# A graph attention layer: the first-tile rows of every batch gathered raw from x and projected in the loop, x and table moved in 4.6 KB pieces

## The chip, the cores and the metric

The kernel runs on one core of one Trainium2 chip. The metric is the device time of one execution in microseconds, the median of several runs. A core has five instruction streams: PE (TensorE, matmuls and transposes), DVE (VectorE), ACT (ScalarE), POOL (GpSimd, which issues the indirect gathers here) and SP (SyncE, which issues most plain DMAs). Each works through its own instructions in order; semaphores order them against each other. PEld in the profile is the loading of weights into TensorE, which runs beside its matmuls.

## The reference

One layer of a graph network with attention: 12,500 nodes of 128 values, 412,500 edges sorted by their target `dst`, 64 values per edge, 4 heads of 32.

```python
h = relu(layernorm(x))                               # per node, eps 1e-5
hn = (h @ W_node.T).reshape(num_nodes, 4, 32)
e = (edge_attr @ W_edge.T).reshape(num_edges, 4, 32)
att = sum(concat([hn[src], hn[dst], e]) * a, -1)     # per edge and head
att = where(att > 0, att, 0.2 * att)
m = maximum(segment_max(att, dst), 0)
ex = exp(att - m[dst])
denom = segment_sum(ex, dst) + (num_edges - deg)[:, None] * exp(-m)
out = x + segment_sum((ex / denom[dst])[:, :, None] * hn[src], dst)
```

All values are float32.

## The kernel before

**The table (the start of the program, lines 185 to 452).** Each node gets a row of 144 float32 in a DRAM table: per head 32 projected values, two ones and the source's part of the logit (35 columns, `AW`), then four target parts of the logit. The 98 tiles of 128 nodes are taken in groups of 3, 6, 9, 9 and so on (`XB = 9`), and each group in units of three tiles (`XS`). A group is loaded by SP (`load_rows`, L254, in the layout "(b p) d -> p b d", where one partition gets nine separate pieces of 512 bytes), measured on DVE (`bn_stats`, L272), normalized (`normalize`: ACT L307, but in the first two units of a group the third tile on DVE, L304), transposed on PE (L313), put through relu on DVE (L318), multiplied by the weights `wall` on PE (L323) and copied to `rows` by ACT (L330), while POOL sets the ones (L331). ACT issues the write of a whole group to the table (L335, 576-byte pieces). The order is written out by hand: in step k unit k is projected, unit k+2 normalized and turned, unit k+8 measured. After that come `extent` on DVE for the four groups of target indices (L236 to L240), eight small matmuls (L413) and a row of DVE operations that make per-chunk constants.

**The loop (lines 774 to 808).** The edges are cut into chunks of 7 tiles of 128 edges; 8 chunks make a batch, so a batch has 56 tiles, and there are 58 batches. Iteration b does, in this order of code:

- `index(b + 2)` and `load(b + 1)`: SP loads of the indices, the edge values `eft` (1,792 KB), the targets `mem` (896 KB) and eight small pieces `twb` of the table;
- `gather(b + 1)`: POOL first copies `sums` into `gate` (L507) and then issues 56 indirect gathers (L509), one per tile, which fetch 128 table rows each into the batch's `hs` buffer. There are two `hs` buffers, one for even and one for odd batches. `sums` is written by ACT (L623) out of the last PSUM group of a scatter, so the copy makes the gathers wait until the scatter that used this `hs` buffer is done;
- `weigh(b)`: when the batch's rows have landed, DVE and ACT turn logits into weights (L568 to L591);
- `scatter(b)`: DVE multiplies the rows by the weights (L605, eight times), PE sums them per target with one-hot matrices `hot` in three groups of chunks (L613: three, three and two chunks, 14 instruction records each) into two PSUM buffers `pa`, and ACT collects each group (L636, 12, 12 and 8 copies; L623 just before the last eight);
- `begin(b + 1)`: DVE compares targets (L536), PE computes the edge part `z` of the logits (L541, 16 records, and L545, 8), DVE makes `key` and `hot` (L549 to L560);
- `merge`, after every second batch: DVE (and two ACT exponentials) chain the collected chunks and add them into `acc` (L640 to L683), with the small PSUM tile `here` (L669, L670) on the way;
- once, at b = 3, `count_windows`, which uses DVE, four loads and four matmuls;
- after about every fourth batch `finish`: the finished nodes' results are normalized and added to x.

The order of the code is the order on each engine (`manual_schedule`): what stands later in this list runs later on its engine, and an instruction that waits holds up all that follow it on the same engine.

## Time and profile before

| what | us |
|---|---|
| median of three runs (lowest, highest) | 4809.41 (4808.47, 4812.89) |
| the profiled execution | 4815.92 |
| its span, first to last instruction | 4814.2 |
| mean granted TensorE clock | 0.643 of full speed |
| first gather of table rows | 74.10 |
| first and last L507 (there are 56) | 233.2, 4700.0 |

Busy times of the engines over the span:

```profile
PE 1946.2 (40%) x4305; PEld 658.6 (14%) x4305; DVE 1805.7 (38%) x3337; ACT 719.1 (15%) x2772; POOL 3073.5 (64%) x3333
```

A line of the groups view reads: source line, engine, operation, what is written and read, how often, then busy time in us and the mean of one in ns, then the time the engine was idle just before these instructions and what ended most of that. "issue" is a wait for nothing that the profile shows, "remote" one whose releaser it doesn't know. A line of the timeline reads: start, duration, engine, line, operation, and in brackets the idle time before it and its releaser. A stage, in what follows, is the time from one L507 to the next.

### The profile page before, as it was taken

To read this page: it belongs to the slowest core of one execution; us is meant where nothing else is said; L and a number is where in the kernel's file an instruction comes from. 1 tells how busy PE (TensorE), PEld (TensorE's weight loads), DVE (VectorE), ACT (ScalarE), POOL (GpSimd) and SP (SyncE) were. 2 spreads that over 40 slices of the span, in tenths; PEclk is the share of its full clock that TensorE was granted. 3 is DMA by queue.
4 is the path that set the end of the run, shared out by engine and by line. 5 is a ranking of instruction groups with operands and counts; after the bars stand their busy time and mean duration, and the time that the engine had idled before them with its cause. 6 is when DMAs were issued, how large, how long until landed. Compare 5 with 4: busy or idle time off the path is not lost.

```text
span 4814.2 us, 21409 instructions
## 1 busy us (share of the span) xinstructions
PE 1946.2 (40%) x4305; PEld 658.6 (14%) x4305; DVE 1805.7 (38%) x3337; ACT 719.1 (15%) x2772; POOL 3073.5 (64%) x3333
## 2 busy tenths in 40 slices
PE   5334343433344335343434443434334433443353
PEld 3111111111011111110111111111111111110012
DVE  6242434242334332433343333424342434242425
ACT  5111111110111111111111111111111111110111
POOL 3666666666666666666666666666666666666662
PEclk8566666666666656665656665666566756666666
DMA  6332433333333333333333333333343333333431
GB/s 189 90 88 73 118 79 100 80 103 78 100 83 101 83 95 84 100 79 100 83 95 88 91 88 94 85 94 89 88 95 79 100 80 99 78 104 76 103 81 51
DMA packets 227639, 440.72 MB, mean 92 GB/s; under 512 B 85394, under 2 KB 135566, under 8 KB 227502
## 3 DMA queue, kind: packets, MB, share of 16 engines
q0 software_dynamic: 103136, 237.83, 21.8%
q1 hardware_dynamic: 111038, 194.10, 13.4%
q10 hardware_dynamic: 13328, 7.36, 0.5%
q14 instruction: 100, 0.82, 0.1%
q8 instruction: 37, 0.61, 0.1%
HBM read 423.75 MB, written 15.29 MB: 91 GB/s over the span
## 4 chain that ended last, share of the span: by engine, by line
issue 29%; another core or an unknown queue 27%; PE 22%; DVE 12%; ACT 8%; DMA 1%; DVEq 0%; SPq 0%; ACTq 0%; POOL 0%
PE pa L613 13%; PE z L541 6%; ACT r L636 4%; PE z L545 3%; DVE up L580 2%; DVE m L582 2%; ACT up L749 1%; DVE z L576 1%; ACT a L577 1%; ACT both L586 1%; DVE acc L683 1%; DVE a L583 1%; DVE up L664 1%; DVE hs L605 1%
## 5 line engine op out<-in xcount | busy, mean ns | idle before, releaser
L509 POOL DMA_INDIRECT hs<-table,ends x3223 | 3054.4, 948 | 1037.3 <-issue 1008.5
L613 PE MATMUL pa<-hs,hot 128*96 128x420 f32 (+2 forms) x2526 | 967.1, 549 | 1606.8 <-issue 1184.7
L560 DVE TENSOR_TENSOR hot<-exr,key 128x448 f32<-128x448 f32 x231 | 137.4, 621 | 2460.3 <-remote 2136.4
L541 PE MATMUL z<-eft,wa 128*32 128x384 f32 (+1 forms) x928 | 587.0, 695 | 913.6 <-issue 913.6
L636 ACT COPY r<-pa 32x35 f32<-32x35 f32 x1842 | 385.0, 209 | 2782.7 <-remote 1965.1
L613 PEld LDWEIGHTS pa<-hs,hot 128*96 128x96 f32 (+2 forms) x2526 | 445.1, 181 | 2152.8 <-issue 2044.2
L605 DVE TENSOR_TENSOR hs<-hs,exr 128x924 f32<-128x924 f32 x461 | 476.8, 1102 | 0.0
L545 PE MATMUL z<-mem,twb 128*32 128x512 f32 x464 | 341.2, 826 | 268.1 <-issue 268.1
L507 POOL COPY gate<-sums 32x1 f32<-32x1 f32 x56 | 9.9, 177 | 567.4 <-ACT sums L623 543.0
L541 PEld LDWEIGHTS z<-eft,wa 128*32 128x32 f32 x928 | 104.4, 117 | 1325.4 <-issue 1325.4
L576 DVE TENSOR_TENSOR z<-z,zst 32x224 f32<-32x224 f32 x232 | 89.8, 387 | 162.0 <-PE z L545 74.1
L586 ACT ACTIVATE both<-a 32x224 f32<-32x224 f32 x232 | 89.9, 388 | 370.7 <-DVE a L583 186.7
L536 DVE TENSOR_TENSOR mem<-mem,exr 128x896 f32<-128x896 int32 x116 | 120.4, 1077 | 65.5 <-issue 48.1
L577 ACT ACTIVATE a<-z 32x224 f32<-32x224 f32 x232 | 80.3, 346 | 418.0 <-issue 274.1
L545 PEld LDWEIGHTS z<-mem,twb 128*32 128x32 f32 x464 | 61.2, 134 | 585.3 <-issue 563.3
L683 DVE TENSOR_TENSOR acc<-acc,a 128x70 f32 x461 | 108.5, 235 | 33.8 <-issue 14.5
L580 DVE TENSOR_TENSOR_SCAN up<-pen,z 32x896 f32<-32x896 f32 x58 | 117.0, 2017 | 2.0
L582 DVE TENSOR_TENSOR_SCAN m<-pen,up 32x896 f32<-32x896 f32 x58 | 116.4, 2007 | 2.0
L588 DVE SCALAR_TENSOR_TENSOR both<-pen,m 32x224 f32<-32x224 f32 x232 | 88.7, 382 | 7.1 <-issue 4.8
L749 ACT COPY up<-a 32x224 f32<-32x224 f32 x208 | 70.7, 340 | 33.6 <-issue 23.3
L578 DVE TENSOR_TENSOR z<-z,a 32x896 f32<-32x896 f32 x58 | 63.0, 1087 | 24.5 <-issue 12.6
L583 DVE TENSOR_TENSOR a<-z,m 32x896 f32<-32x896 f32 x58 | 62.5, 1078 | 2.0
(142 smaller groups left out, 726.0 us busy)
## 6 DMA issues: line engine op xcount, KB each, us to landing
eft<-in_ef SPq DMA_DIRECT2D x58, 1792.0 KB
mem<-in_dstc SPq DMA_DIRECT2D x58, 896.0 KB
hs<-table,ends POOLq DMA_INDIRECT x3223
twb<-table SPq DMA_DIRECT2D x464, 0.5 KB
pen<-pens SPq DMA_DIRECT2D x58, 112.1 KB
table<-rows ACTq DMA_DIRECT2D x9, 648.0 KB
xg<-in_x SPq DMA_DIRECT2D x13, 448.0 KB
out<-xg SPq DMA_DIRECT2D x13, 448.0 KB
```

Source lines behind the costliest of these rows:

```text
L509: by_itself(nc.gpsimd.indirect_dma_start(out=s.hs[:, i, :], out_offset=None, in_=table[:, :], in_offset=bass.IndirectOffsetOnAxis(ap=s.end ...
L541: nc.tensor.matmul(s.z[:, part], wa3[:, j, :], s.eft[:, j, part], start=(j == 0), stop=False)
L545: nc.tensor.matmul(s.z[:, part], twb[:, s.b % 2, k, :], s.mem[:, k, part], start=False, stop=(k == 1))
L560: nc.vector.tensor_tensor(hot[:, :, q0:q0 + 2, :].rearrange("p t q r -> p q t r"), rows_ps[:, None, None, :].to_broadcast([P, 2, T, W]), k ...
L576: nc.vector.tensor_tensor(grouped(s.z, g), grouped(s.z, g), zst[g * R:(g + 1) * R, :, :], op=OP.add)
L580: nc.vector.tensor_tensor_scan(up, s.pen[:, :CE], s.z, 0.0, op0=OP.add, op1=OP.max)
L582: nc.vector.tensor_tensor_scan(m[:, ::-1], s.pen[:, CE:0:-1], up[:, ::-1], 0.0, op0=OP.add, op1=OP.max)
L586: nc.scalar.activation(both[g * R:(g + 1) * R, 0, :, :], grouped(att, g), AF.Exp)
L605: nc.vector.tensor_tensor(rows, rows, ex_ps[:, :n, q * H:(q + 1) * H, None].to_broadcast([P, n, H, HB]), op=OP.mult)
L613: nc.tensor.matmul(pa[:v * W, :v * H * AW], hot[:, i, q0:q0 + v, :].rearrange("p q r -> p (q r)"), by_chunk[:, q0:q0 + v, i, :], start=(i ...
L636: nc.scalar.copy(to, pa[q * W:(q + 1) * W, k:k + AW])
L683: nc.vector.tensor_tensor(cols, cols, put[:, i0 + i, :, :], op=OP.add)
```

## The change

Tile number 2 (`FIRST`) of each batch is no longer gathered from the table in the loop: `gather` issues 55 gathers instead of 56. Instead POOL gathers, while the table is built, the raw x rows of that tile for all 58 batches into `xs`, with the host-made index array `ahead`. DVE measures them (`measure_drawn`) after the extents, and SP writes them to a DRAM buffer `drawn` in two halves. In the loop `load` brings one batch's 128 rows back; `normalize` (ACT, and a PE transpose) stands before `begin(b + 1)`, `project` (DVE relu and a matmul) behind it, and `keep_rows` (DVE) writes the rows into `hs` after the merge. The transposed tile, the projected rows and merge's `here` share one PSUM tile `spare`.

Around it: x is loaded and the table written in the layout "(p b) d -> p b d", where a partition gets nine neighbouring rows (4.6 KB of x); POOL's memsets of pens, rows and xg go to DVE, or are dropped; DVE normalizes one tile per group of nine instead of two; the target indices for `extent` are loaded later, at k = 24, and into two buffers.

```diff
@@ -56,6 +56,7 @@
 LOGIT = EROW * 4
+FIRST = 2
 EPS = 1e-5
@@ -106,6 +107,7 @@
     ends: bass.AP,
+    ahead: bass.AP,
     dstc: bass.AP,
@@ -123,6 +125,7 @@
     pens = dram.tile([NC2, CE + 1], F32, name="pens")
+    drawn = dram.tile([P, NBT, D], F32, name="drawn")
 
@@ -148,6 +151,9 @@
     wa3 = const.tile([P, SB, R], F32, name="wa3")
+    wall = const.tile([P, ROW], F32, name="wall")
+    drawn_rstd = const.tile([P, NBT], F32, name="drawn_rstd")
+    drawn_shift = const.tile([P, NBT], F32, name="drawn_shift")
     ext = const.tile([P, NG, 2], F32, name="ext")
@@ -188,6 +194,8 @@
     ):
+        which = p1.tile([P, NBT], I32, name="which")
+        nc.scalar.dma_start(which, ahead)
         wn = p1.tile([P, D], F32, name="wn")
@@ -214,25 +222,47 @@
         nc.gpsimd.memset(wa3, 0.0)
-        wall = p1.tile([P, ROW], F32, name="wall")
         nc.gpsimd.memset(wall, 0.0)
 
-        rises, pens_sb = [], []
-
-        def load_extents():
-            for g in range(NG):
+        pen_bufs = [p1.tile([P, CE + 1], F32, name=f"pen{g}") for g in range(NG)]
+        line = {what: p1.tile([P, NC2], F32, name=what) for what in ("low", "top", "off", "qn", "bm", "later", "last")}
+        xs = p1.tile([P, NBT, D], F32, name="xs")
+        for b in range(NBT):
+            nc.gpsimd.indirect_dma_start(
+                out=xs[:, b, :], out_offset=None, in_=x[:, :],
+                in_offset=bass.IndirectOffsetOnAxis(ap=which[:, b:b + 1], axis=0))
+
+        def keep_drawn(first, last):
+            nc.sync.dma_start(drawn[:, first:last, :], xs[:, first:last, :])
+
+        def measure_drawn():
+            stats = p1.tile([P, NBT, 2, 3], F32, name="drawn_stats")
+            for b in range(NBT):
+                nc.vector.bn_stats(stats[:, b, :, :].rearrange("p a b -> p (a b)"), xs[:, b, :])
+            tot = p1.tile([P, NBT, 2], F32, name="drawn_tot")
+            nc.vector.tensor_tensor(tot, stats[:, :, 0, 1:], stats[:, :, 1, 1:], op=OP.add)
+            dif = p1.tile([P, NBT], F32, name="drawn_dif")
+            nc.vector.tensor_tensor(dif, stats[:, :, 0, 1], stats[:, :, 1, 1], op=OP.subtract)
+            nc.vector.scalar_tensor_tensor(dif, dif, D / 4.0, dif, op0=OP.mult, op1=OP.mult)
+            nc.vector.tensor_tensor(dif, dif, tot[:, :, 1], op=OP.add)
+            nc.scalar.activation(drawn_rstd, dif, AF.Sqrt, bias=eps, scale=1.0 / D)
+            nc.vector.reciprocal(drawn_rstd, drawn_rstd)
+            nc.vector.scalar_tensor_tensor(drawn_shift, tot[:, :, 0], -0.5, drawn_rstd, op0=OP.mult, op1=OP.mult)
+
+        loaded = []
+
+        def load_extents(first, last):
+            for g in range(first, last):
                 n = min(P, NC2 - g * P)
-                dch = p1.tile([P, CE], I32, name=f"dch{g}")
+                dch = p1.tile([P, CE], I32, name="dch", bufs=2)
                 nc.sync.dma_start(dch[:n, :], dstc[g * P:g * P + n, :])
-                rise = p1.tile([P, CE - 1], I32, name=f"rise{g}")
-                pen = p1.tile([P, CE + 1], F32, name=f"pen{g}")
-                nc.gpsimd.memset(pen, -BIG)
-                rises.append((dch, rise))
-                pens_sb.append(pen)
+                loaded.append(dch)
 
...
             n = min(P, NC2 - g * P)
-            (dch, rise), pen = rises[g], pens_sb[g]
+            dch, pen = loaded[g], pen_bufs[g]
+            rise = p1.tile([P, CE - 1], I32, name="rise")
+            nc.vector.memset(pen[:, ::CE], -BIG)
             nc.vector.tensor_tensor(rise[:n, :], dch[:n, 1:], dch[:n, :CE - 1], op=OP.subtract)
@@ -251,10 +281,10 @@
             s.x = p2.tile([P, XB, D], F32, name="xg", bufs=5)
-            nc.sync.dma_start(s.x[:, :full, :],
-                              x[b0 * P:(b0 + full) * P, :].rearrange("(b p) d -> p b d", p=P))
+            s.order = "(p b) d -> p b d" if full == n else "(b p) d -> p b d"
+            nc.sync.dma_start(s.x[:, :full, :], x[b0 * P:(b0 + full) * P, :].rearrange(s.order, p=P))
             if full < n:
-                nc.gpsimd.memset(s.x[:, full, :], 0.0)
+                nc.vector.memset(s.x[:, full, :], 0.0)
                 rest = N - (b0 + full) * P
@@ -300,7 +330,7 @@
                 k = slice(u.i0 + i, u.i0 + i + 1)
-                if i == XS - 1 and u.i0 < 2 * XS:
+                if i == XS - 1 and u.i0 < XS:
                     nc.vector.tensor_scalar(u.hn[:, i, :], s.x[:, k, :].rearrange("p b d -> p (b d)"),
@@ -328,11 +358,11 @@
             nc.scalar.copy(rows, u.ph[:, :u.m, :])
-            nc.gpsimd.memset(rows[:, :, :EROW].rearrange("p b (h k) -> p b h k", h=H)[:, :, :, HD:HD + 2], 1.0)
+            nc.vector.memset(rows[:, :, :EROW].rearrange("p b (h k) -> p b h k", h=H)[:, :, :, HD:HD + 2], 1.0)
             return s if u is s.units[-1] else None
...
         def write(s):
-            nc.scalar.dma_start(table[s.b0 * P:(s.b0 + s.n) * P, :].rearrange("(b p) c -> p b c", p=P),
+            nc.scalar.dma_start(table[s.b0 * P:(s.b0 + s.n) * P, :].rearrange(s.order, p=P),
                                 s.rows[:, :s.n, :])
@@ -393,7 +423,9 @@
                 early = [index(b) for b in range(2)]
-                load_extents()
+            if k == 24:
+                load_extents(0, 2)
+                keep_drawn(0, NBT // 2)
             k += 1
@@ -406,17 +438,20 @@
             extent(g)
+            load_extents(g + 2, min(g + 3, NG))
+        keep_drawn(NBT // 2, NBT)
+        measure_drawn()
         pb = [pps.tile([P, NC2], F32, name=f"pb{k}", bufs=1) for k in range(2)]
...
                                  ident[:n, :n], start=True, stop=True)
-        low = p1.tile([P, NC2], F32, name="low")
+        low = line["low"]
         nc.vector.tensor_copy(low, pb[0])
-        top = p1.tile([P, NC2], F32, name="top")
+        top = line["top"]
         nc.vector.tensor_tensor_scan(top, low, low, 0.0, op0=OP.max, op1=OP.max)
-        off = p1.tile([P, NC2], F32, name="off")
+        off = line["off"]
         nc.vector.tensor_tensor(off, low, top, op=OP.is_lt)
@@ -465,6 +500,11 @@
     nc.scalar.copy(nid_ps, nid)
+
+    spare = ps.tile([P, 512], F32, name="here")
+    here_ps = spare[:, :MC * 2].rearrange("p (c j) -> p c j", j=2)
+    turned_ps = spare[:, MC * 2:MC * 2 + P]
+    row_ps = spare[:, MC * 2 + P:MC * 2 + P + ROW]
 
@@ -489,6 +529,8 @@
                 f"twb{s.b}", twb_sems, twb_done, s.b % 2)
+        s.drawn = work.tile([P, D], F32, name="drawn")
+        nc.sync.dma_start(s.drawn, drawn[:, s.b, :])
         s.hs = (work if s.b % 2 else even).tile([P, SB * CT, ROW], F32, name="hs")
@@ -497,7 +539,8 @@
                     if t < held[c]:
-                        s.tiles.append(i)
+                        if i != FIRST:
+                            s.tiles.append(i)
                     else:
@@ -510,6 +553,24 @@
                 f"rows{s.b}", row_sems, row_done, s.b % ROWSEMS)
+
+    def normalize(s):
+
+        both = work.tile([P, BUF], F32, name="m")
+        s.hn, s.hT = both[:, :D], both[:, D:2 * D]
+        nc.scalar.activation(s.hn, s.drawn, AF.Identity, scale=drawn_rstd[:, s.b:s.b + 1],
+                             bias=drawn_shift[:, s.b:s.b + 1])
+        nc.tensor.transpose(turned_ps, s.hn, ident)
+
+    def project(s):
+
+        nc.vector.tensor_scalar(s.hT, turned_ps, 0.0, None, op0=OP.max)
+        nc.tensor.matmul(row_ps, s.hT, wall, start=True, stop=True)
+
+    def keep_rows(s):
+
+        nc.vector.tensor_copy(s.hs[:, FIRST, :], row_ps)
+        nc.vector.memset(s.hs[:, FIRST, :EROW].rearrange("p (h k) -> p h k", h=H)[:, :, HD:HD + 2], 1.0)
 
@@ -666,7 +727,7 @@
         put = work.tile([P, BUF], F32, name="a")[:, :MC * 2 * AW].rearrange("p (c j d) -> p c j d", c=MC, j=2)
-        here = ps.tile([P, MC, 2], F32, name="here")[:, :n, :]
+        here = here_ps[:, :n, :]
         nc.vector.tensor_copy(here, lastm[:, c0:c0 + n, :])
@@ -696,7 +757,7 @@
         nc.vector.tensor_copy(more, far)
-        row = ps.tile([1, NC2], F32, name="here")
+        row = ps.tile([P, BANKS * 512], F32, name="up")[0:1, :NC2]
         for g in range(NG):
@@ -793,12 +854,16 @@
             if b + 1 < NBT:
+                normalize(batch(b + 1))
                 begin(batch(b + 1))
+                project(batch(b + 1))
             if b >= 0:
...
                 del batches[b]
+            if b + 1 < NBT:
+                keep_rows(batch(b + 1))
             if b == 3:
@@ -1043,6 +1108,7 @@
+        "ahead": np.ascontiguousarray(s.reshape(NBT, SB * CT, P)[:, FIRST, :].T),
```

More of the change, by code (lines that the diff above doesn't have):

```diff
@@ L430 @@
         nc.vector.tensor_copy(q0, bl[0:1, :])
-        qn = p1.tile([P, NC2], F32, name="qn")
+        qn = line["qn"]
         nc.vector.tensor_copy(qn, bl)
-        bm = p1.tile([P, NC2], F32, name="bm")
+        bm = line["bm"]
         nc.vector.tensor_scalar(bl, bi, W - 1, None, op0=OP.bitwise_and)
         nc.vector.tensor_copy(bm, bl)
-        later = p1.tile([P, NC2], F32, name="later")
+        later = line["later"]
         nc.vector.tensor_scalar(later, bm, rcol, None, op0=OP.is_gt)
@@ L441 @@
         nc.vector.tensor_tensor(new[:, 1:], qn[:, 1:], qn[:, :NC2 - 1], op=OP.not_equal)
-        last = p1.tile([P, NC2], F32, name="last")
+        last = line["last"]
         nc.vector.memset(last, 1.0)
```

## The prediction

> **What bounds the kernel now.** I read the costliest groups of the page first, then the timeline of one stage engine by engine, then the times from one L507 to the next.
>
> In the costliest groups (busy us, mean ns of one, then the idle time before them and what ended it) POOL's gathers lead, and two idle times stand out: POOL waits 543.0 us for the ACT copy L623, and the ACT copies of the scatter wait on nothing that the profile can name.
>
> ```profile
> L509 POOL DMA_INDIRECT hs<-table,ends x3223 | 3054.4, 948 | 1037.3 <-issue 1008.5
> L636 ACT COPY r<-pa 32x35 f32<-32x35 f32 x1842 | 385.0, 209 | 2782.7 <-remote 1965.1
> L507 POOL COPY gate<-sums 32x1 f32<-32x1 f32 x56 | 9.9, 177 | 567.4 <-ACT sums L623 543.0
> ```
>
> The timeline of POOL in the stage from 2023.25 to 2103.61 (start, duration, and in brackets the idle time before) shows a gather about every 1.25 us, the last one at 2093.43, and then 9.24 us of waiting.
>
> ```profile
> 2023.25 0.18 POOL L507 COPY gate<-sums 32x1 f32<-32x1 f32 x1 [11.69 <-ACT sums L623]
> 2024.06 0.97 POOL L509 DMA_INDIRECT hs<-table,ends  x1 [0.63 <-issue]
> ...
> 2092.18 0.94 POOL L509 DMA_INDIRECT hs<-table,ends  x1 [0.30 <-issue]
> 2093.43 0.94 POOL L509 DMA_INDIRECT hs<-table,ends  x1 [0.30 <-issue]
> 2103.61 0.18 POOL L507 COPY gate<-sums 32x1 f32<-32x1 f32 x1 [9.24 <-ACT sums L623]
> ```
>
> What it waits for is the third scatter group (I call the three groups of L613 g1, g2, g3). PE starts g3 at 2055.56, yet ACT gets g2's result at 2091.36 and g3's at 2103.40:
>
> ```profile
> 2040.62 13.05 PE L613 MATMUL pa<-hs,hot 128*96 128x420 f32 x28 [15.62 <-DVE hs L605]
> 2055.56 3.52 PE L613 MATMUL pa<-hs,hot 128*64 128x280 f32 x14 [1.88 <-ACT r L636]
> 2059.00 2.76 PE L541 MATMUL z<-eft,wa 128*32 128x512 f32 x6
> 2062.65 0.59 PE L541 MATMUL z<-eft,wa 128*32 128x512 f32 x1 [0.89 <-issue]
> 2065.46 0.59 PE L541 MATMUL z<-eft,wa 128*32 128x512 f32 x1 [2.22 <-issue]
> 2068.25 0.80 PE L541 MATMUL z<-eft,wa 128*32 128x384 f32 x1 [2.20 <-issue]
> ```
> ```profile
> 2052.87 2.64 ACT L636 COPY r<-pa 32x35 f32<-32x35 f32 x12 [16.57 <-remote]
> 2091.36 2.64 ACT L636 COPY r<-pa 32x35 f32<-32x35 f32 x12 [35.86 <-remote]
> 2103.40 0.15 ACT L623 COPY sums<-pa 32x1 f32<-32x1 f32 x1 [9.40 <-remote]
> ```
>
> Read together: under a gather PE finishes a first burst (g1) at once, and then only one instruction per 1.4 us: a matmul and its weight load every 2.8 us, and g2's 28 instructions (14 records of each) 38.5 us after g1. It comes free when the gathers are done. Over the stages that moment is the first gather's start + 56 x 1.416 us, some 9 us after POOL's last one. I call it the drain. Nothing like it appears after 4740, where no gather runs. DVE does the same after 14 small memsets in the stage that began at 475.0, in the middle of its gathers:
>
> ```profile
> 507.07 0.19 DVE L716 MEMSET up<- 1x1 f32 x14
> 512.50 0.63 DVE L717 TENSOR_TENSOR both<-q,up 1x464 f32<-1x464 int32 x1 [5.24 <-remote]
> 513.90 0.62 DVE L719 TENSOR_REDUCE more_f<-both 1x1 f32<-1x464 f32 x1 [0.77 <-DVE both L717]
> 515.30 0.14 DVE L720 TENSOR_SCALAR more_f<-more_f 1x1 f32<-1x1 f32 x1 [0.78 <-DVE more_f L719]
> ```
>
> The span is 233.2 (start to the first L507) + 55 stages of 81.21 mean (233.2 to 4700.0) + 114.2 = 4814.2. Stages are 80.4 when g1 starts some 17.5 us after L507, 80.8 at 29.5, 82.95 at 38.7, and once 86.16, at 68 (count_windows). The first is the drain itself (0.8 + 56 x 1.416 = 80.1) + 0.3; in the third g2 too is freed only at the drain, which costs 2.85 for g3; in the last g1 has barely finished at it, 6.1 after 80.1.
>
> **The change, part by part.**
>
> *One gather less per batch.* Issue: 58 x (0.948 + 0.30) = 72 us less on POOL. But the drain goes by 1.416, so a stage falls to 0.8 + 55 x 1.416 = 78.7 at the drain, 1.4 less each, 55 x 1.4 = 78 less, if all else keeps its place.
>
> *Normalize, transpose and project in the loop.* ACT normalizes one 128x128 tile (0.39 to 0.49 in L307's rows), PE transposes it (0.33 in L313's), DVE relus, PE projects, DVE copies and sets ones, about 0.2 to 0.6 each: under 3 us of busy time per batch on engines busy under 41%. What matters is their place. ACT's normalize stands behind the copies of g3 (L636, 1.75 us), so it can't run before the drain. The PE transpose waits for it and stands ahead of next batch's z (L541, L545) on PE's queue. Before, z ran behind g3 during the trickle and was complete at the drain: its last record is at 2103.25, and weigh can start as L507 does. Now after the drain: 1.9 (copies) + 0.45 + 0.5 (transpose and hand over) + 8.17 (L541's 16 records, at 107.23) + 3 to 4 (L545) = 14 to 15 us, all of it after L507 and under the next gathers. Only then do project and keep_rows run, and weigh waits for keep_rows on DVE. From weigh's first instruction to g1 are 16.3 us in every stage (13.5 to 29.8, 22.4 to 38.7). So g1 starts near 31 instead of 17.5 in a batch without merge. In a merge batch DVE's copy into `here` now shares a PSUM tile with turned and row and waits for project; the remaining 8 of the merge's 13 us come after, and g1 is near 39 instead of 29.5. That is the least delay. With it g2 comes at the drain, and each stage is 78.7 + 2.85 = 81.55: the gain of the gather is given back, +0.3 a stage, 55 x 0.34 = +19.
>
> The dearer bound is the trickle. The z that now falls under the gathers has 2 + 32 + 16 instructions (records and weight loads) in one burst, project 8 more. In the stages above only some 28 to 31 pass before 1.4 us each sets in: g1's 28, and 0 to 3 of g2's. (At 107.23 32 passed in 8.17 us under a gather, but the next 16 came 15 us later.) Then 20 of z take 28 us more: project at 40, or 51 with its own 8, and g1 at 57 to 67, in a merge batch 8 later. g1 has 28 instructions again, so it too is freed only at the drain, as in the stage of 86.16: 78.7 + 6.5 = 85.2, +4.0 a stage, 55 x 4.0 = +219. The late merge batches may go beyond (g1 at 75 + 18 to the end of g3 = 93, in half of the stages: +8 x 27 = +216 more at the worst). I take 85.2, since the burst of 50 is nearer to g1 + g2 (56 in a row, of which the second half trickled) than to any burst that did not.
>
> *58 gathers at the start.* POOL is nearly free there (9.17 of the first 74 us), DVE and ACT are not:
>
> ```profile
> 0.00:74.00 74.00, 51.31 (x301) 42.19 (x301) 60.92 (x255) 51.52 (x124) 9.17 (x54) 0.95 0.74 217
> ```
>
> (The columns are the stretch, its length, PE, PEld, DVE, ACT, POOL with instruction counts, clock, DMA share, GB/s.) 58 gathers from about 5 us are issued by 5 + 72 = 77 and drained at 5 + 58 x 1.416 = 87; the first table gather, now at 74.10, stands behind them on POOL and so behind its queue: at least +3 to +13. The upper bound is the trickle again: 18 PE records per 3-tile unit in 1.65 us now; under the gathers nearly all of the 33 units would wait, and some 30 x 1.65 = 50 us of it follow the drain, so that the table is ready near 137 instead of 71 (+60). I take +50, nearer to the upper end because it is the same law as in the loop. 15 gathers from 74.10 to 96.76, beside DVE's extents, took 1.51 us each instead of 1.25; at that rate the issue alone is 58 x 1.51 = 88 us, +15, which lies within these bounds.
> The Trainium skill ("SBUF — State Buffer", two separate sides) says that descriptors of a GpSimd DMA can't be written while DVE is in a two-port mode, which speaks against putting gathers beside the busiest DVE stage; the row at 74 to 97 agrees in sign (1.51 against 1.25), and by it the start costs +15.
>
> *The rest.* 58 bn_stats (3 took 0.67: 13 us on DVE) stand in the tail of the start, where gathers of batch 0 already run: hidden unless DVE is late for batch 0's begin (which waits there until 128.71 now), +0 to +13, inside the +50. POOL's memsets move to DVE: 33 x 0.12 = 4 us; one normalize of 0.34 per group moves to ACT, 11 x 0.44 = 5 us; the 4.6 KB pieces of x and table against 512 B: DMA share 0.74, not full, so -5 to 0. Nothing net. SP gets one 64 KB load per batch behind twb: eft and mem of a batch have tens of us of slack. Tail: +5 (z later by 15 in a stretch of 114).
>
> **Sum.** 233.2 + 50 + 55 x 85.2 + 119 = 5088 of span, +1.7 outside it as now (4815.92 against 4814.2), and 6.5 less for the median (4809.41): 5083. I say 5085.
>
> **Rivals.**
> 1. *Given back, not more*: z passes under the early gathers without trickle, stages 81.55. 233.2 + 12 to 50 + 55 x 81.55 + 118 = 4848 to 4886, so 4845 to 4885. For it: the unslowed L541 at 107.23; while POOL has issued few gathers, little is queued. Against it: g2.
> 2. *Faster*: the drain decides alone. Its place is L507, its price -1.4 a stage; it decides if g2 is complete before the drain, that is if g1 starts before about 29, or if the shorter interference frees PE sooner. Stages 79.0 to 79.8: 233.2 + 12 to 50 + 4345 to 4389 + 116 = 4706 to 4788. For it: the stages at 17.5 stand at the drain + 0.3. Against it: the transpose ahead of z.
> 3. *Merge batches go past the drain*: up to 93 in half of the stages, 5083 + up to 216 = 5150 to 5300. For it: the shared PSUM tile; against it: in none of the 55 stages is g1 later than 68.
>
> **How the numbers follow.** The forecast (5040 to 5130 on its own) has 0.45, rival 1 0.24, rival 2 0.22, rival 3 0.09. The bound of no change is 0.2%, 10 us, about what a measurement of this kernel can tell. Faster: rival 2 less its upper edge, 0.21; same 0.04, from the edge of rivals 1 and 2; slower 0.75. The range leaves out the fast end of rival 2 and the top of rival 3: 4770 to 5230.
>
> **What would show it.** Right: weigh's first transpose 40 or more after L507, L541's records 2.8 apart just after L507, g2 and g3 freed together at 78.7, stages near 85, first table gather past 110. Rival 1: L541 in 8 to 9 us, stages 81.5. Wrong: stages below 80, or z before normalize.

## The result, and the profile after

The changed kernel takes 4919.41 us (median of four runs, 4916.85 to 4920.36), the kernel before 4808.94 beside it: ratio 1.0228, interval 1.021 to 1.0246. It is slower by 110 us. The profiled execution took 4916.85, its span is 4914.7, and its parts say where:

| stretch of the span | before | after | difference |
|---|---|---|---|
| start to the first gate copy (L507, now L550) | 233.2 | 346.3 | +113.1 |
| 55 stages, mean | 81.21 | 80.56 | -35.9 in all |
| last gate copy to the end | 114.2 | 137.5 | +23.3 |

The loop gained a little; the start and the end lost. (The sum is +100.5. The two profiled executions lie 7.0 above and 2.6 below their medians, and 0.4 more lies outside the span; that is the rest of the 110.5.)

The costliest groups of the changed kernel that answer to those shown of before (L509, L636, L507 have become L552, L697, L550):

```profile
L552 POOL DMA_INDIRECT hs<-table,ends x3165 | 2997.2, 947 | 1072.4 <-issue 996.3
L697 ACT COPY r<-pa 32x35 f32<-32x35 f32 x1842 | 384.9, 209 | 2184.8 <-remote 1529.1
L550 POOL COPY gate<-sums 32x1 f32<-32x1 f32 x56 | 9.9, 177 | 659.9 <-ACT sums L684 659.9
```

POOL issues 58 table gathers less (2997.2 against 3054.4 busy), but waits 659.9 instead of 543.0 for `sums`. The timelines of PE and ACT in the stage from 1968.39 to 2047.84, one without a merge:

```profile
1970.56 0.47 PE L563 MATMUL here<-ident,m 128*128 128x128 f32 x1 [11.96 <-ACT m L561]
1970.96 7.64 PE L602 MATMUL z<-eft,wa 128*32 128x512 f32 x16
1978.43 3.17 PE L606 MATMUL z<-mem,twb 128*32 128x512 f32 x8
1981.53 0.51 PE L568 MATMUL here<-wall,m 128*128 128x144 f32 x2
1998.83 12.94 PE L674 MATMUL pa<-hs,hot 128*96 128x420 f32 x28 [16.79 <-issue]
```
```profile
2012.76 2.63 ACT L697 COPY r<-pa 32x35 f32<-32x35 f32 x12 [18.10 <-PE pa L674]
2044.96 2.64 ACT L697 COPY r<-pa 32x35 f32<-32x35 f32 x12 [29.56 <-remote]
2047.63 0.15 ACT L684 COPY sums<-pa 32x1 f32<-32x1 f32 x1
```

z (L602, L606) does stand behind the transpose and now runs under the early gathers, but in 11 us, without a pause. PE's row of 28 records is g1 and g2 together, and its records run straight through; what is late is the result as ACT gets it. g1 is collected 14 us after its start, g2 32 us later, at 76.6 of the stage, and g3 at 79.2: the drain, 78.7, and half a us. So nearly all stages without a merge take 79.3 to 79.6. With a merge they take 80.8 to 81.3, since g1 starts at 48 or 58 there.

One stage stands apart, the one with `count_windows`: it takes 98.67, where it took 86.16 before. Under its gathers DVE's small memsets come one per 1.4 us, so weigh is late, and g1 starts 82.6 after L550, behind the drain (a line of DVE's timeline, then one of PE's):

```profile
631.54 0.06 DVE L777 MEMSET up<- 1x1 f32 x1 [1.34 <-issue]
668.91 15.76 PE L674 MATMUL pa<-hs,hot 128*96 128x420 f32 x42 [43.33 <-DVE hs L666]
```

Without this stage the mean of the other 54 is 80.23, against 81.12 before.

The start is where the time went. PE's timeline from 24.76 on, with the gathers of raw rows running from 3.88 and drained, by 58 x 1.416, at 86:

```profile
24.76 1.65 PE L353 MATMUL ph<-wall,hT 128*128 128x144 f32 x6
40.68 1.24 PE L343 MATMUL pt<-ident,hn 128*128 128x128 f32 x3 [14.27 <-ACT hn L337]
48.74 1.81 PE L353 MATMUL ph<-wall,hT 128*128 128x144 f32 x6 [6.82 <-issue]
65.18 1.25 PE L343 MATMUL pt<-ident,hn 128*128 128x128 f32 x3 [14.63 <-issue]
73.93 1.81 PE L353 MATMUL ph<-wall,hT 128*128 128x144 f32 x6 [7.50 <-issue]
...
86.42 1.65 PE L353 MATMUL ph<-wall,hT 128*128 128x144 f32 x6
87.86 0.85 PE L343 MATMUL pt<-ident,hn 128*128 128x128 f32 x3
```

One unit (three records of transposes and six of multiplications) in 24 to 25 us instead of 1.65, until the drain. POOL's timeline then has the first table gather at 143.35 (74.10 before), a gap of 23 us ahead of the second batch's gathers, and the first gate copy:

```profile
143.35 0.94 POOL L552 DMA_INDIRECT hs<-table,ends  x1 [67.18 <-DVE pen L267]
...
234.84 0.95 POOL L552 DMA_INDIRECT hs<-table,ends  x1 [23.11 <-issue]
...
346.32 0.18 POOL L550 COPY gate<-sums 32x1 f32<-32x1 f32 x1 [43.12 <-ACT sums L684]
```

The gap has the same cause on DVE. `measure_drawn` has 58 bn_stats; 26 run at once, and the others, now beside the first table gathers, one every 1.4 us. The per-chunk constants behind them are done at 232.6, and the second batch's gathers, which start at 234.84, seem to wait for these:

```profile
156.03 5.11 DVE L241 BATCH_NORM_STATS2 drawn_stats<-xs 128x6 f32<-128x128 f32 x26
161.53 0.29 DVE L241 BATCH_NORM_STATS2 drawn_stats<-xs 128x6 f32<-128x128 f32 x1 [0.38 <-issue]
162.91 0.29 DVE L241 BATCH_NORM_STATS2 drawn_stats<-xs 128x6 f32<-128x128 f32 x1 [1.09 <-issue]
```

### The profile page after: what moved, and what is told of

Read it like the earlier page. It is cut to its first block, busy times and chain, and to the rows that moved or that the text cites. A ratio compares the mean times of both kernels' runs of the same rounds, so it can differ in the third digit from the quotient of the medians.

```text
span 4914.7 us, 22169 instructions
## 1 busy us (share of the span) xinstructions
PE 1798.9 (37%) x4479; PEld 719.8 (15%) x4479; DVE 1848.6 (38%) x3602; ACT 750.8 (15%) x2842; POOL 3063.8 (62%) x3295
## 4 chain that ended last, share of the span: by engine, by line
another core or an unknown queue 33%; issue 25%; PE 16%; DVE 12%; ACT 11%; DVEq 1%; DMA 1%; ACTq 0%; SPq 0%
PE pa L674 8%; ACT r L697 7%; PE z L602 6%; PE z L606 2%; DVE up L641 2%; DVE m L643 1%; ACT both L647 1%; DVE z L637 1%; ACT a L638 1%; DVE acc L744 1%; ACT up L810 1%; DVE a L644 1%; DVE hs L666 1%; DVE a L735 1%
## 5 line engine op out<-in xcount | busy, mean ns | idle before, releaser
L552 POOL DMA_INDIRECT hs<-table,ends x3165 | 2997.2, 947 | 1072.4 <-issue 996.3
L674 PE MATMUL pa<-hs,hot 128*96 128x420 f32 (+2 forms) x2526 | 1037.1, 581 | 1872.7 <-issue 1244.7
L674 PEld LDWEIGHTS pa<-hs,hot 128*96 128x96 f32 (+2 forms) x2526 | 472.6, 192 | 2420.8 <-issue 2271.0
L697 ACT COPY r<-pa 32x35 f32<-32x35 f32 x1842 | 384.9, 209 | 2184.8 <-remote 1529.1
L602 PE MATMUL z<-eft,wa 128*32 128x384 f32 (+1 forms) x928 | 470.5, 672 | 0.0
L563 PE MATMUL here<-ident,m 128*128 128x128 f32 x58 | 27.2, 469 | 1098.8 <-ACT m L561 995.0
L550 POOL COPY gate<-sums 32x1 f32<-32x1 f32 x56 | 9.9, 177 | 659.9 <-ACT sums L684 659.9
L606 PE MATMUL z<-mem,twb 128*32 128x512 f32 x464 | 183.9, 539 | 0.0
L563 PEld LDWEIGHTS here<-ident,m 128*128 128x128 f32 x58 | 10.4, 180 | 1128.2 <-ACT m L561 1024.2
L602 PEld LDWEIGHTS z<-eft,wa 128*32 128x32 f32 x928 | 116.0, 131 | 326.9 <-issue 326.7
L572 DVE COPY hs<-here 128x144 f32<-128x144 f32 x58 | 17.6, 304 | 347.7 <-PE here L568 183.4
L637 DVE TENSOR_TENSOR z<-z,zst 32x224 f32<-32x224 f32 x232 | 89.8, 387 | 134.2 <-issue 82.2
```

The lines of the kernel that those rows point to most:

```text
L552: by_itself(nc.gpsimd.indirect_dma_start(out=s.hs[:, i, :], out_offset=None, in_=table[:, :], in_offset=bass.IndirectOffsetOnAxis(ap=s.end ...
L602: nc.tensor.matmul(s.z[:, part], wa3[:, j, :], s.eft[:, j, part], start=(j == 0), stop=False)
L606: nc.tensor.matmul(s.z[:, part], twb[:, s.b % 2, k, :], s.mem[:, k, part], start=False, stop=(k == 1))
L637: nc.vector.tensor_tensor(grouped(s.z, g), grouped(s.z, g), zst[g * R:(g + 1) * R, :, :], op=OP.add)
L674: nc.tensor.matmul(pa[:v * W, :v * H * AW], hot[:, i, q0:q0 + v, :].rearrange("p q r -> p (q r)"), by_chunk[:, q0:q0 + v, i, :], start=(i ...
L697: nc.scalar.copy(to, pa[q * W:(q + 1) * W, k:k + AW])
```

## The experiments

They went to several chips of the same type, and the chips differ: beside some runs the kernel before took 4810 to 4819, as in the recorded result, beside others 4161 to 4175. I call the first kind A and the second kind B. No chip was seen as both, so the chip is the nearest reading of the difference; what in it differs was not found. The first two runs told of here show what differs; the four of the next part ran before them. Each time is to be read against the kernel before on its own chip.

**The two kernels unchanged, on a chip of kind B.** No edit.

> The kernel before, unchanged, for a trace beside the others: the last four kernels ran on a chip on which it took 4164.35 instead of 4808.94. Theory (on that chip the gathers are served faster than POOL issues them, so nothing trickles and a stage is POOL's 56 x 1.25 = 70): stages 70 to 70.5, first L507 near 216 if first gathers start at 74, the whole 4160 to 4170. If instead the chip is like the first one: stages 81.2, 4805 to 4816. Rival for the difference (a faster TensorE clock or other compute): stages that are not 56 x 1.25.

> The changed kernel, unchanged. Theory: what it does hangs on how fast the chip serves gathers. Where POOL's issue is the bound, one gather less is 58 x 1.25 = 72 less, and the start costs 5 to 20: 4095 to 4115 against 4164, ratio 0.984 to 0.988. Where they drain at 1.416: 4915 to 4921 against 4809, as recorded. Rival (the loss at the start is there on every chip, +113, and the four kernels were faster for the part that each changed): 4200 or more against 4164.

4161.31, and 4111.18 against 4161.68: ratio 0.988 (0.9863 to 0.9898). Both totals are those of the first theory. On this chip the change is a gain of 1.2%. A stage of the kernel before is 70.08, which is 56 x 1.25, the chain of waits is POOL's own, and ACT's copies of the scatter wait for PE by name:

```profile
POOL hs L509 73%; PE pa L613 1%; DVE stats L272 0%; DVE hT L318 0%; POOL gate L507 0%; DVE hn L304 0%; PE ph L323 0%; DMA xg<-in_x 0%; DVE up L580 0%; DVE m L582 0%; PE pt L313 0%; POOLq L509 0%; DVE z L576 0%; ACT both L586 0%; DVE acc L683 0%
...
L509 POOL DMA_INDIRECT hs<-table,ends x3223 | 3052.1, 947 | 976.7 <-issue 973.0
L636 ACT COPY r<-pa 32x35 f32<-32x35 f32 x1842 | 385.3, 209 | 823.4 <-PE pa L613 803.7
```

Nothing trickles: idle time of 823.4 instead of 2782.7 for the same copies, and in the changed kernel g1 is collected 7.6 us after its start (2032.30 to 2039.90) instead of 14. TensorE's clock is not the difference: z's 16 records L602 take 7.60 us here and 7.64 there. The stretches of the changed kernel there against the kernel before's: start +4.3 (215.3 to 219.6), 55 stages of 68.83 instead of 70.08, -68.8 in all, end +9.5 (89.8 to 99.2). The stretch from 20 to 60 us, by engines (start to end, length, PE, PEld, DVE, ACT, POOL busy with instructions, clock, DMA share, GB/s), first the changed kernel on the chip of the result (kind A), then on this one:

```profile
20.00:40.00 20.00, 1.91 (x7) 1.57 (x7) 0.81 (x2) 0.28 (x1) 15.10 (x16) 0.54 0.25 64
40.00:60.00 20.00, 3.05 (x9) 2.00 (x9) 1.50 (x7) 1.39 (x4) 15.10 (x16) 0.50 0.22 52
```
```profile
20.00:40.00 20.00, 15.46 (x99) 11.67 (x98) 16.58 (x82) 17.30 (x46) 15.10 (x16) 1.00 0.81 268
40.00:60.00 20.00, 15.94 (x101) 12.28 (x102) 16.87 (x83) 17.22 (x44) 15.10 (x16) 1.00 0.89 317
```

The same 16 gathers by POOL in each 20 us; 7 matmul records beside them, or 99.

**Parts of the change, on that chip of kind B** (kernel before there 4164.35). The gathers alone, added to the kernel before:

```diff
+        xs = p1.tile([P, NBT, D], F32, name="xs")
+        for b in range(NBT):
+            nc.gpsimd.indirect_dma_start(out=xs[:, b, :], out_offset=None, in_=x[:, :], ...)
...
-                nc.gpsimd.memset(pen, -BIG)
+                nc.vector.memset(pen, -BIG)
...
```

> The kernel before, with the 58 gathers of raw x rows added at the start and nothing else of the change in the loop (their rows are not used); the build's memsets stand on DVE so that they don't queue behind the gathers. Theory (while gathers run, PE, DVE and ACT get on by one instruction per 1.4 us once a first burst is used up): the build stands still until the drain at about 4 + 58 x 1.416 = 86, the first table gather comes near 140 instead of 74.1, the whole is 60 to 70 longer, 4870 to 4880. Rival (only POOL's queue counts, 58 x 1.248 = 72): first table gather at 77 to 90, the whole 4812 to 4825.

4195.69, +31: the totals expected belong to the other kind of chip, and the first table gather, at 112.60, is neither theory's. The last unit reached the table's buffer at 82.75, some 15 later than in the kernel before (68.04), and the gather then waited for the constants too (the copy of `nid` at 111.74). In the kernel before and in the changed kernel it does not wait for these. I take it for a side effect of the added buffer, which was not tested. So the price is an upper bound for this chip.

Three more, each the changed kernel with one edit: two plain loads of other rows in place of the 58 gathers, wide statistics, and z first:

```diff
-        for b in range(NBT):
-            nc.gpsimd.indirect_dma_start(out=xs[:, b, :], ...)
+        for b in range(0, NBT, 29):
+            nc.scalar.dma_start(xs[:, b:b + 29, :], x[b * P:(b + 29) * P, :].rearrange(...))
```
```diff
-            for b in range(NBT):
-                nc.vector.bn_stats(stats[:, b, :, :]..., xs[:, b, :])
+            nc.vector.tensor_reduce(tot, xs, AX.X, OP.add)
+            nc.scalar.activation(xs, xs, AF.Square)
+            nc.vector.tensor_reduce(dif, xs, AX.X, OP.add)
...
```
```diff
-                normalize(batch(b + 1))
                 begin(batch(b + 1))
+                normalize(batch(b + 1))
```

> The changed kernel with the 58 gathers at the start replaced by two plain loads of as many rows of x (other rows, so the first tile of each batch is computed from wrong nodes). Theory of the trickle: the first table gather falls from 143.35 to 75 to 85 and the whole by 60 to 70, to 4850 to 4860; the 58 bn_stats beside the first table gathers still trickle, so the first L550 stays some 40 later than in the kernel before. Rival (the 4.6 KB layout, the moved memsets or the later loads of target indices are what delays the table): first table gather still past 110.

> The changed kernel with the 58 bn_stats and their sums replaced by two wide reductions on DVE and one wide square on ACT (10 instructions in place of 65). Theory (DVE's many small instructions trickle under the first table gathers, 1.4 us each from the 27th on): the per-chunk constants end before 205 instead of 232.6, the second batch's gathers follow the first's without the 23 us gap, the first L550 comes at 300 to 325 instead of 346.3, the whole is 20 to 45 less, 4875 to 4900. Rival (the first weigh waits for the loads of drawn rows and targets, which come late anyway): first L550 within 5 us of 346, the whole 4915 to 4920.

> The changed kernel with begin (the edge part z) ahead of normalize and its transpose on PE, as z stood before. My prediction priced z behind the transpose at +0.3 to +4.0 a stage; the measured stage is 80.58. Theory A (the place of z costs through weigh's later start): weigh starts near 6 after L550 instead of 14 in batches without merge, g1 at 22 instead of 30; stages without merge stay at the drain, 79.0 to 79.4, stages with merge fall from 80.9 to 79.5 to 80.3, mean 79.2 to 79.9, the whole 4845 to 4885. Theory B (z under the early gathers passes free, and under the late ones it uses up what g2 needs): stages rise, mean 80.8 to 82, the whole 4930 to 4995.

4113.21, 4110.75 and 4105.32, one run each: all within 6 of the changed kernel's 4111.18, whose own runs lie 6 apart, with stages of 68.8. Where POOL's issue is the bound, none of these parts is worth more than that, and these three runs tell nothing of the recorded loss. The first table gather came at 83.18 even without the 58 gathers (80.50 with them, 71.74 in the kernel before). So on such a chip those 9 us are hardly the gathers' doing, though the plain loads may have a cost of their own.

**Layout, and an attempt to make gathers slow** (kernel before there 4175.01). The new layout alone in the kernel before; the old one in the changed kernel; and in both an added load per batch:

```diff
+                junk = work.tile([P, 97, 4], F32, name="junk")
+                nc.scalar.dma_start(junk, x[:97 * P, :4].rearrange("(b p) h -> p b h", p=P))
```

> The kernel before with x loaded and the table written in pieces of nine rows per partition, and nothing else of the change. On the chip where the kernel before takes 4161.68: theory (the build is bound by DVE and ACT, the pieces matter only for the first load): first table gather 70 to 72 against 71.74, the whole 4158 to 4163. Rival (the many 512-byte pieces hold up the loads): first table gather 60 to 67, the whole 4150 to 4156.

> The changed kernel with the old layout, 512-byte pieces of x and 576-byte pieces of the table. Same chip: theory (with 58 gathers beside them the loads of x share the DMA engines, and small pieces make that worse): first table gather 3 to 30 later than in the changed kernel, the whole 4112 to 4140 against 4111.18. Rival (the layout is worth nothing): first table gather within 2, the whole 4105 to 4114.

> The kernel before with one added load per batch from ACT's queue, 12,416 pieces of 16 bytes, which nothing reads; it is to make the gathers' transfers slower than POOL issues them, as they were in the recorded runs. Theory (what was seen there, PE, DVE and ACT getting on by one instruction per gather, comes of gathers that are served slower than issued): stages above 75, with g2's result near the end of the gathers instead of 30 after L507. Rival (the slow service is nothing that other transfers make): stages 70 to 71, g2 at 30 to 35.

> The changed kernel with the same added load. Theory: stages longer than without it (68.82), by about as much as in the kernel before, z still right after the drain, and weigh behind it at 14 to 38 as in the recorded trace; the stage is then within 1.5 of the kernel before's. Rival: stages 68.8 to 69.5.

Each was run once. The new layout in the kernel before: 4170.48, that is 4.5 less, with the first table gather at 72.54. The old layout in the changed kernel: 4119.26, with the first table gather at 84.16. That is 8.4 more than the changed kernel with the new layout and the added load took on the same chip (4110.84, first table gather 81.52), but 0.987 of the kernel before, as the changed kernel was 0.988 on the other chip. So the layout is worth at most some 8 us, 0.2%, and single runs don't tell that from nothing. The added loads, 4169.44 and 4110.84, left the stages at 70.3 and 68.8: that much other traffic does not make gathers slow, and what does stays open.

**A rearranged version.** Its first form was tried on the chip of the first two runs. Normalize stands ahead of the scatter, project behind z, keep_rows ahead of merge, merge's `here` lies in another PSUM bank, and the wide statistics stand behind the per-chunk constants:

> The changed kernel with wide reductions for the statistics, behind the per-chunk constants; normalize and its transpose ahead of the scatter, project behind z, and keep_rows ahead of merge; merge's small tile in another PSUM bank. Where POOL's issue is the bound: stages 68.8 as in the last three, the start at its least, 4090 to 4105. Where gathers drain at 1.416: stages 79.0 to 79.8, first L550 near 300, 4780 to 4815, about the time of the kernel before. Rival: the order of the loop doesn't matter there and only the start gains, 4860 to 4880.

4108.21, 3 above the range expected, ratio 0.9873 (0.9855 to 0.989): a tie with the changed kernel. Its end was still 98.5: keep_rows, now ahead of merge, waits 12.0 for project on DVE. In the second form project stands ahead of z and keep_rows behind merge; against the changed kernel:

```diff
...
+    here_ps = bank[:, T * R + W + GB * 4 + NC2 // 4:].rearrange("p (c j) -> p c j", j=2)
...
+                if b + 1 < NBT:
+                    normalize(batch(b + 1))
                 scatter(s)
             if b + 1 < NBT:
-                normalize(batch(b + 1))
+                if b >= 0:
+                    project(batch(b + 1))
                 begin(batch(b + 1))
-                project(batch(b + 1))
...
```

> As the kernel called combined, but project stands ahead of z and keep_rows behind merge again, since in the traces where POOL's issue is the bound the changed kernel's last batches wait for them: the time from the last L550 to the end was 99.2 against 89.7 in the kernel before (merge's write of here waited for project). Theory: that stretch falls to 89 to 92, stages stay 68.8, the whole is 8 to 12 below the changed kernel, ratio to the kernel before 0.984 to 0.987. Where gathers drain at 1.416: 4780 to 4815. Rival (the end is set by the last gathers and their scatter alone): the stretch stays near 98, ratio 0.987 to 0.988.

This one came to a chip of kind A: 4831.37 against 4810.06, ratio 1.0044 (1.003 to 1.0057), still 0.4% slower, but 88 less than the changed kernel on its chip of kind A. Its first gate copy, on POOL, is 44 earlier although its first table gather is not:

```profile
142.72 0.94 POOL L551 DMA_INDIRECT hs<-table,ends  x1 [66.65 <-DVE pen L266]
...
302.29 0.18 POOL L549 COPY gate<-sums 32x1 f32<-32x1 f32 x1 [19.86 <-ACT sums L683]
```

The gap ahead of the second batch's gathers is gone; the constants end at 168.9, and two wide reductions do not trickle:

```profile
167.63 1.26 DVE L483 TENSOR_SCALAR nid<-top,rcol 32x116 f32<-32x116 f32 x4
168.92 7.89 DVE L240 TENSOR_REDUCE drawn_tot<-xs 128x58 f32<-128x7424 f32 x1
183.26 7.89 DVE L243 TENSOR_REDUCE drawn_dif<-xs 128x58 f32<-128x7424 f32 x1 [6.46 <-ACT xs L241]
```

The end is 112.6 instead of 137.5. The stages are 80.25 instead of 80.56 in the mean, but nearly all of that is the stage with `count_windows`, 85.92 instead of 98.67: the other 54 have a mean of 80.15 against 80.23. And z is back behind g3, where it trickles again (its records lie between some 50 and 84 of a stage). So neither place of z makes a clear difference in this loop. The total was above the range expected because the stages were (80.25 where 79.0 to 79.8 had been expected); the first gate copy, expected near 300, came at 302.3.

**Spacing the gathers.** The kernel of the second form with two edits: only 40 of the 58 batches are served from the start (NX), and the gathers go in bursts of five (BURST), where a POOL copy of the last row makes each burst wait for the one before:

```diff
-        for b in range(NBT):
+        for b in range(NX):
+            if b and b % BURST == 0:
+                nc.gpsimd.tensor_copy(seen, xs[:, b - 1, 0:1])
             nc.gpsimd.indirect_dma_start(out=xs[:, b, :], ...)
```

> The kernel combined_2 with 40 of the 58 batches taken so, and the gathers at the start in bursts of 5, each burst waiting until the one before has landed. Where gathers drain at 1.416: theory (an engine has a budget of completions that a gather-free moment fills again; 5 gathers are 7 us, some 77 PE instructions of the build): the build goes on under the gathers, first table gather at 80 to 95, the whole 4780 to 4805, below the kernel before. Rival (each gather stops the build for 1.2 however they are spaced, 40 x 1.2 = 48): first table gather near 120, the whole 4820 to 4840. Where POOL's issue is the bound: 18 gathers more in the loop, 4110 to 4125.

First on a chip of kind B: 4119.96 against 4164.65, ratio 0.9892 (0.9876 to 0.9909), stages of 68.9 and, from the batch on that has 56 gathers again, 70.1. Then:

> The kernel combined_bursts, unchanged, once more, since its first run came to a chip on which POOL's issue is the bound. The theories and their numbers are the same: where gathers drain at 1.416, first table gather at 80 to 95 and the whole 4780 to 4805 if a gather-free moment fills the budget, first table gather near 120 and the whole 4820 to 4840 if each gather stops the build however they are spaced; where POOL's issue is the bound, 4115 to 4125.

A chip of kind A: 4802.05 against 4819.19, ratio 0.9966 (0.9952 to 0.9979). Both figures are the first theory's. The gain is 0.3% on kind A and 1.1% on kind B; the changed kernel lost 2.3% on kind A and gained 1.2% on kind B. POOL's timeline of one burst and what follows, and the same stretches by engines as above:

```profile
31.79 0.18 POOL L235 COPY seen<-xs 128x1 f32<-128x1 f32 x1 [4.92 <-DMA xs<-in_x,which]
32.47 0.97 POOL L236 DMA_INDIRECT xs<-in_x,which  x1 [0.50 <-issue]
...
40.68 0.18 POOL L235 COPY seen<-xs 128x1 f32<-128x1 f32 x1 [2.24 <-DMA xs<-in_x,which]
...
86.57 0.94 POOL L557 DMA_INDIRECT hs<-table,ends  x1 [6.70 <-DVE pen L271]
```
```profile
20.00:40.00 20.00, 14.84 (x88) 12.00 (x88) 13.80 (x68) 14.51 (x37) 9.87 (x12) 0.91 0.66 217
40.00:60.00 20.00, 14.35 (x78) 11.18 (x79) 13.87 (x69) 14.88 (x39) 9.91 (x12) 0.91 0.68 210
```

88 matmul records beside 12 entries on POOL (10 gathers and 2 copies), where 16 gathers in an unbroken row left 7. First table gather 86.57 instead of 142.72, first gate copy 245.1 instead of 302.3. That there are 18 gathers fewer explains at most part of it: at 1.416 each, an unbroken row of 40 would have put the first table gather near 117 (an estimate from 142.72). The stages, with 40 of 58 batches relieved, have a mean of 80.80.

**What could not be told.** Two kernels were to settle the trickle on a chip of kind A: the changed kernel with eight idle matmuls more per batch, and the second form above with plain loads for the gathers.

> The changed kernel with 8 matmuls more behind project in each batch (32 instructions with their weight loads, into a part of PSUM that nothing reads). Where gathers drain at 1.416: theory (a budget: some 85 to 95 PE instructions complete freely after the drain, now 54 of transpose, z and project, 28 of g1 and some 5 of g2, and only then 1.4 us each): with 32 more g1 itself trickles, its result comes at 60 to 75 instead of 44.4 in stages without merge, the mean stage rises by 2 to 5, the whole is 5030 to 5190. Rival (the trickle sets in with the second scatter group, whatever ran before it): g1's result at 44 to 48, stages within 0.5, the whole 4915 to 4945. Where POOL's issue is the bound: 4105 to 4125, no difference.

> The kernel combined_2 with the 58 gathers at the start replaced by two plain loads of other rows (the first tile of each batch is then computed from wrong nodes). Where gathers drain at 1.416: theory (the start is longer only because the build stands still under those gathers): first table gather 76 to 86 instead of 142.72, the whole 4760 to 4775 against 4831.37. Rival (layout, memsets and later loads make part of it): 4785 or more. Where POOL's issue is the bound: 4098 to 4110.

Both came to chips of kind B, twice each: 4111.48 and 4110.76; 4100.49 and 4105.62, against 4164.65 and 4165.09. There they show no more than that 32 PE instructions a batch are free. Their question is open.

## Why the prediction was right and wrong

*The drain* held as a law: a stage without merge is 0.8 + 55 x 1.416 and some 0.7 more. *The direction* held too, but half by luck: of the +276 forecast, +219 lay in the loop, and the loop gained 35.9. The kernel is slower for the start and the end.

*The step that failed* is "I take 85.2", the price of +4.0 a stage for z behind the transpose: that z's 50 instructions under the gathers would use up the burst, so that g1 starts at 57 to 67. Transpose, z and project passed in 11 us without a pause, and g1 started 30.4 after L550, the prediction's own least delay. The stages are 80.56, -0.65, where the sum had +4.0: 255 us between the two. Even the lower price, +2.85 above the drain, was too dear for a stage without merge: there g2 came 2.1 us ahead of the drain.

The threshold, 28 to 31 instructions, was drawn from stages of the kernel before, in which z runs right up to the drain. In the changed kernel PE is idle before the drain, and 2 + 48 + 4 instructions of transpose, z and project pass, then g1's 28 (slowed, in 14 us), and some 5 of g2 (an estimate: 32 us at 1.4 leave 23 of its 28). A burst that idle time fills again would fit both; it was not shown. The prediction had a row that spoke against its threshold, 32 instructions of z in 8.17 us at 107.23, and set it aside because the next 16 came 15 us later. But the same pause, 15.79, stands in the kernel before on kind B, where nothing trickles, so it is not the trickle's.

The measured mean lies between the rivals' stages, 79.0 to 79.8 and 81.55: the stages without merge are those of *Faster*, the ones with merge nearly those of *Given back*. In a merge batch DVE's copy into `here` waits 7.8 for project, and g1 is late. *Merge batches go past the drain* happened in one stage only, that with `count_windows`.

*The start* was mis-sized: +50 in the sum, +113 measured. Its upper bound had the right mechanism, the build standing still until the drain and 50 us of it left then: the table near 137 instead of 71. That is +66, not the +60 written beside it, and the first table gather is 69.3 later. That an unbroken row of gathers stops the build is shown by the burst run, where spaced gathers did not, though the 58 were never taken out alone on a chip of kind A. What I had priced "+0 to +13, inside the +50", the 58 bn_stats, was the rest, 44: I had the trickle in hand and did not apply it to these. The wide statistics, in the second form, gave 44 back (together with the other edits of that form).

*The end*: +5 forecast, +23.3 measured, and most of it is the trickle once more. Behind the merge DVE sets 25 tiles of `hs` that hold no edges to zero. In the kernel before they pass in 3.95 us (the first line); in the changed kernel the merge first waits for z and project on PE, and of the memsets eight pass and the rest come one per 0.7 to 2.1 us, until 4820.77:

```profile
4713.17 3.95 DVE L502 MEMSET hs<- 128x144 f32 x25
```
```profile
4791.09 0.20 DVE L731 COPY here<-lastm 128x32 f32<-128x32 f32 x1 [6.51 <-PE z L606]
...
4799.05 1.28 DVE L545 MEMSET hs<- 128x144 f32 x8
4800.84 0.18 DVE L545 MEMSET hs<- 128x144 f32 x1 [0.51 <-issue]
4802.93 0.18 DVE L545 MEMSET hs<- 128x144 f32 x1 [1.92 <-issue]
```

The memsets take 21.7 us, 17.8 more than before. On the chip of kind B they pass in 3.95 in the changed kernel too, and what is left there, +9.5, can be read on DVE in its last merge, which waits 6.25 for project behind z:

```profile
4044.00 0.19 DVE L728 COPY carry<-up 128x34 f32<-128x34 f32 x1
4050.44 0.18 DVE L731 COPY here<-lastm 128x16 f32<-128x16 f32 x1 [6.25 <-PE here L568]
```

The second form, with its own tile and an early project, ends in 112.6 on its chip of kind A, where the memsets pass in 4.2. The burst version, of the same form, ends in 113.7 on kind A and in 88.3 on kind B (114.2 and 89.8 in the kernel before).

*The cheap edits* were rightly put near nothing: the layout is worth at most 0.2% on a chip of kind B; on kind A none of them was tried alone. *The naive price*, 58 x 1.248 = 72, is about what the loop gains where POOL's issue is the bound: 68.8 over 55 stages. I had not listed that the drain itself could hang on the chip.

On the chip of kind B POOL issued its 58 gathers at 1.25 each beside a DVE busy 83% of the time (16.58 of 20 us), so nothing of the +15 at 1.51 each was seen at the start. The Trainium skill ("SBUF — State Buffer", two separate sides), which had been put beside that price, says that descriptors of a GpSimd DMA can't be written while DVE is in a two-port mode. The trace doesn't show which of DVE's operations were in one, so this is no test of the rule.

## What to carry to other kernels

Before a stage is priced by the busy time of its engines, look for what gets on by one step per transfer. On some chips many small instructions beside an unbroken row of gathers go at the gathers' pace, here 1.4 us each, and this holds for the start and the end of a program as much as for its loop: it made the transposes, the 58 statistics and the 25 memsets of this kernel dear. A threshold read from one order of work needn't hold in another. What helped here was to put background gathers in short bursts that wait for their landing, and to replace a row of small instructions beside gathers by a few wide ones. And measure on more than one chip: here the sign of a change of 1 to 2% depended on it.

## What the runs showed of the hardware

The same kernel before took 4808.94, 4810.06 and 4819.19 on three occasions and 4161 to 4175 on the others. On the first kind of chip a long row of gathers takes 1.416 us for each (stages of 79.4 with 55 of them, 80.4 with 56), and PE and DVE, once a first burst has passed, get on by one instruction per gather. On the other kind POOL's issue, 1.25 us, is the bound: 70.08 with 56. The transfers' own time doesn't explain it: the gathers' queue kept the 16 DMA engines busy for 21.8% of 4814.2, that is 0.33 us per gather, and for 22.2% of 4159.5, 0.29. What holds the instructions back, how long the first burst is, and why bursts of five gathers do not show it and 58 in a row do, is open.
